# A graph network's edges as one list in units of 17 chunks, instead of 18 padded chunks for each tile

## The chip, the cores and the metric

The kernel runs on one core of one Trainium2 chip. The metric is the device time of one execution in microseconds. Before the change three runs took 12551.64 to 12556.44 us, median 12553.1 us.

Five engines work side by side, each through its own instructions in order: TensorE (PE; its weight loads are PEld), VectorE (DVE), ScalarE (ACT), GpSimd (POOL) and SyncE (SP, which here only starts transfers).

## What is computed

A graph has 12,500 nodes with 128 features each, and 212,500 edges (100,000 pairs in both directions, and one self-loop per node), sorted by their destination `dst`. Four blocks run in turn, each on the normalized and rectified features and each added back to them; cut to what matters:

```
L0: two graph attention convolutions (128 -> 64 -> 128):
    e     = leaky_relu(alpha_src[src] + alpha_dst[dst], 0.2)
    ex    = exp(e - segment_max(e, dst)[dst])
    out   = segment_sum(ex / segment_sum(ex, dst)[dst] * h[src], dst)
L1: a transformer convolution, 8 heads of 16, and a feed-forward part:
    alpha = (q[dst] . k[src]) / sqrt(16)          (per head)
    a     = softmax of alpha over the edges of one dst
    out   = segment_sum(a * v[src], dst) + x @ Wskip, then Wo, norm, 128->512->128, norm
L2: out   = segment_max over the edges of (x[src] @ Ws + edge_weight * ww), then two dense layers
L3: out   = segment mean of h[src]
```

Five of these steps (two in L0, one each in L1, L2, L3) read a row of a table for every edge and reduce over the edges of a node. They are the five edge passes: gat1, gat2, attn, max, sum.

## The kernel before, in words

Nodes are cut into 98 tiles of 128. Each tile owns a padded list of `C = 18` chunks of 128 edges, from the first edge of its first node on; what lies beyond its last node is left out of the sums by its position. A tile that does not fit is flagged and recomputed by a slow loop (`listed`); with these inputs no tile is flagged, and the slow loop runs zero times.

The first stage ("prologue") checks the sorting, loads weights, and prepares the lists: for each tile, three transfers from a row offset held in a register (L339 to L341) fetch 18 x 128 source indices, destinations and weights; `IDX` holds the sources, `first_d` marks where a node's edges begin, `feat_d` and `last_d` hold five rows per tile from which one matrix product gives the squared distance between an edge's destination and each node. Then `before_gat1` makes the first table `t1`. The features stay in SBUF as `X` throughout.

`edge_pass` (L905) runs one pass. `gather` (L858) issues, one tile ahead, 18 indirect transfers on POOL's queue; each fetches 128 table rows into one chunk of a buffer `g` of `G = 6` chunks. A tile part then works in two halves, the second half beside the first half of the next tile, and a `post` generator makes the dense work of a finished tile (`after_gat1` and so on). The generators fix only the order in which the work is written down; a scheduler of the framework then orders each engine's instructions at build time by its own cost estimates, and places the waits.

- `per_node` (L875) and `per_edge` (L885) turn the distances into 0/1 matrices `st` (node by edge) and `se` (edge by node): a product on PE, one ACT instruction over 6 chunks.
- In gat1 and gat2, `st` spreads the node's own term to its edges (L996), `node_max` (L948) finds the maximum over each node's edges by a forward and a backward scan (L961, L965), the rows are multiplied by the exponential (L1024), split into three bf16 parts (`split`, L480: two ACT casts, two DVE subtractions), and summed per node by PE with `se` (`aggregate`, L895).
- In attn, `st` spreads the queries (L1063), DVE multiplies and reduces (L1067, L1070), ACT exponentiates, DVE multiplies the values in place in `g` (L1085), and `aggregate` works in f32.
- In max, PE turns the rows and adds the weight term (L1116, L1120), DVE scans (L1124), PE turns back (L1135), the result is split and summed. In sum the rows go straight into `aggregate`.

PSUM has eight banks: two buffers `big` of two banks each for all one-hot, query, transposed and scanned values, two for `mm`, one each for `ex` and `acc`.

Of the kernel before, what the change touches and what calls it, by code (L numbers as in the profile page):

```python
# [18 lines left out]
N = 12500  # L19
# [12 lines left out]
C = 18  # L32
G = 6
NG = C // G
ET = C * P
GW = G * P

# [5 lines left out]
EP = E + ET + 4  # L43

FE = ET + 2 * P + 1

D3 = 3 * D + 2
GT = 7
XW = D + H
BIG = 1.0e30  # L50
# [6 lines left out]
def gnn_kernel(ctx, tc, a, out):  # L57
# [17 lines left out]
    feat_d = dram.tile([T, 5, ET], BF16, name="feat_d")  # L75
    last_d = dram.tile([T, 5, ET], BF16, name="last_d")
    ewf_d = dram.tile([T, 3, ET], BF16, name="ewf_d")
    first_d = dram.tile([T, FE], BF16, name="first_d")
# [4 lines left out]
    tkv = dram.tile([NP, 2 * D], F32, name="tkv")  # L83
# [22 lines left out]
    X = const.tile([P, T, D], F32, name="X")  # L106
# [4 lines left out]
    IDX = const.tile([P, C, T], I32, name="IDX")  # L111

    FIRST = const.tile([P, C, T], BF16, name="FIRST")
# [74 lines left out]


    V.memset(X[:, T - 1, :], 0.0)  # L190
    x_in = a["x"]
    for t0 in range(0, T - 1, GT):
        t1_ = min(t0 + GT, T - 1)
        SY.dma_start(X[:, t0:t1_, :],
                     x_in[t0 * P:t1_ * P, :].rearrange("(t p) c -> p t c", p=P))
    SY.dma_start(X[:LAST, T - 1, :], x_in[(T - 1) * P:N, :])
# [117 lines left out]
    with tc.tile_pool(name="csr", bufs=1) as cp:  # L314
# [16 lines left out]
        ROWI = cp.tile([1, T1], I32, name="ROWI")  # L331
        V.tensor_copy(ROWI, rowr)


        rs_ = cp.tile([T, ET], F32, name="raw_s")
        rd_ = cp.tile([T, ET + 1], F32, name="raw_d")
        re_ = cp.tile([T, ET], F32, name="raw_e")
        for t in range(T):
            r = nc.values_load(ROWI[0:1, t:t + 1], engines=(SPQ,), min_val=0, max_val=E)  # L339
            for o, s, n in ((rs_, src_e, ET), (rd_, dst_e, ET + 1), (re_, ew_e, ET)):  # L340
                SY.dma_start(o[t:t + 1, :], s[ds(r, n), :].rearrange("n o -> o n"))  # L341
        for c in range(C):
            px = psum([P, P], "mm", "px")
            PE.transpose(px[:, :T], rs_[:, c * P:(c + 1) * P], ident[:T, :T])
            V.tensor_copy(IDX[:, c, :], px[:, :T])
        with tc.tile_pool(name="csr_w", bufs=1) as wp:
            for i, x in enumerate(three(wp, re_, [T, ET], "ew")):
                SY.dma_start(ewf_d[:, i, :], x)


        long_ = cp.tile([T, 1], F32, name="long_")
        tn1 = cp.tile([P, 1], F32, name="tn1")
        V.tensor_scalar_mul(tn1, tn, -1.0)
        with tc.tile_pool(name="csr_d", bufs=1) as dp:
            ch = dp.tile([T, ET + 1], F32, name="ch")
            V.memset(ch[:, 0:1], 1.0)
            V.tensor_tensor(ch[:, 1:], rd_[:, 1:], rd_[:, :ET], ALU.not_equal)
            m = dp.tile([T, FE], BF16, name="m")
            V.memset(m[:, :P], 0.0)
            V.memset(m[:, P + ET + 1:], 0.0)  # L360
            V.tensor_scalar_mul(m[:, P:P + ET + 1], ch, -BIG)
            SY.dma_start(first_d, m)
            for c in range(C):
                pc_ = psum([P, P], "mm", "pc_")
                PE.transpose(pc_[:, :T], ch[:, c * P:(c + 1) * P], ident[:T, :T])
                V.tensor_copy(FIRST[:, c, :], pc_[:, :T])
            o1 = dp.tile([T, ET], BF16, name="o1")
            V.tensor_tensor(o1[:, P:], rd_[:, P:ET], rd_[:, :ET - P], ALU.is_equal)
            V.tensor_reduce(long_, o1[:, P:], AX.X, ALU.max)
            dl = dp.tile([T, ET], F32, name="dl")  # L370
            V.tensor_scalar(dl, rd_[:, :ET], tn1[:T, :], FAR, op0=ALU.add, op1=ALU.min)
            V.memset(o1, 1.0)
            for o in (feat_d, last_d):
                hi, lo = square(dp, dl, [T, ET], "q")
                xb = dp.tile([T, ET], BF16, name="xb")
                V.tensor_copy(xb, dl)
                for k, y in enumerate((o1, o1, xb, hi, lo)):
                    SY.dma_start(o[:, k, :], y)
                if o is feat_d:
                    V.scalar_tensor_tensor(dl, dl, -FAR, ch[:, 1:], op0=ALU.add, op1=ALU.mult)  # L380
                    V.tensor_scalar_add(dl, dl, FAR)
# [7 lines left out]
        V.tensor_scalar(flag, flag, float(ET), None, op0=ALU.is_gt)  # L389
# [72 lines left out]
    def act_norm(t):  # L462
        h = w_([P, D], "hn")
        S.activation(h, X[:, t, :], AF.Relu, bias=NM[:, t:t + 1], scale=RS[:, t:t + 1])
        return h

    def pre(t):
        yield from norm(X[:, t, :], RS[:, t:t + 1], NM[:, t:t + 1])
        return act_norm(t)
# [55 lines left out]
    def run(gens, width):  # L525

        gens, live = list(gens), []
        while gens or live:
            while gens and len(live) < width:
                live.append(gens.pop(0))  # L530
            live = [g for g in live if next(g, live) is not live]


    def before_gat1(t):
        hT = yield from transposed((yield from pre(t)))
        yield from gat_begin(t, hT, w1x, HID, t1)

    run((before_gat1(t) for t in range(T)), 2)
# [9 lines left out]
    def after_gat2(t, r):  # L548
        o = gat_end(r, D, b02)
        V.tensor_add(X[:, t, :], X[:, t, :], o)  # L550
        yield
        hT = yield from transposed((yield from pre(t)))
# [3 lines left out]
        r = w_([P, 3 * D], "qkv")  # L556
        V.tensor_add(r, pm[:, :3 * D], bqkv)
        V.tensor_scalar_mul(r[:, :D], r[:, :D], float(HD) ** -0.5)
        q3 = work.tile([P, 3 * D], BF16, name="q3_")
        split(q3, r[:, :D], D, w_([P, D], "rest"))  # L560
        SY.dma_start(tq[rows(t), :], q3)
        SY.dma_start(tkv[rows(t), :], r[:, D:])

    def after_attn(t, r):
        z = w_([P, H], "zh")
        V.tensor_scalar_add(z, r[:, D:], SM_EPS)
        V.reciprocal(z, z)
        agg = w_([P, D], "agg")
        V.tensor_mul(agg.rearrange("p (h d) -> p h d", h=H),
                     r[:, :D].rearrange("p (h d) -> p h d", h=H),  # L570
                     z.unsqueeze(2).to_broadcast([P, H, HD]))
        hn = act_norm(t)
# [45 lines left out]
        V.tensor_add(X[:, t, :], X[:, t, :], u)  # L618
# [3 lines left out]
        hT = yield from transposed((yield from pre(t)))  # L622
# [7 lines left out]
    def after_max(t, r):  # L630
        hT = yield from transposed(act_norm(t))
# [23 lines left out]
        V.tensor_add(X[:, t, :], X[:, t, :], u)  # L655
        yield
        yield from norm(X[:, t, :], RS[:, t:t + 1], NM[:, t:t + 1])
        h3 = work.tile([P, D3], BF16, name="h3")
        split(h3[:, :3 * D], act_norm(t), D, w_([P, D], "rest"))
# [4 lines left out]
    def after_sum(t, r):  # L664
        z = w_([P, 1], "z")
        V.tensor_scalar_max(z, r[:, D:D + 1], 1.0)
        V.reciprocal(z, z)  # L667
        o = w_([P, D], "o")
        V.scalar_tensor_tensor(o, r[:, :D], z, X[:, t, :], op0=ALU.mult, op1=ALU.add)  # L669
# [8 lines left out]
    def listed(table, c, begin, chunk, wid, ew=False, dt=F32):  # L678


        with tc.tile_pool(name="loop", bufs=1) as lp, tc.tile_pool(name="edge", bufs=1) as ed:
            acc = lp.tile([P, D], F32, name="l_acc")
# [96 lines left out]
    def attn_listed():  # L779
        def begin(t, st):  # L780
# [3 lines left out]
            V.memset(st["s"], 0.0)  # L784
            V.memset(st["m"], -BIG)

            def end():
                V.tensor_copy(st["res"][:, :D], st["acc"])
                V.tensor_copy(st["res"][:, D:], st["s"])
            return end  # L790

        def chunk(g, mk, ng, st):
            m, s, acc, q, ed = st["m"], st["s"], st["acc"], st["q"], st["ed"]
# [16 lines left out]
            cs = ed.tile([P, H], F32, name="csh")  # L810
            V.reduce_sum(cs, over_slots(e), AX.X)
            V.tensor_mul(s, s, corr)
            V.tensor_add(s, s, cs)
            v4 = v.rearrange("p k (h d) -> p k h d", h=H)
            V.tensor_mul(v4, v4, e.unsqueeze(3).to_broadcast([P, K, H, HD]))
            red = ed.tile([P, D], F32, name="red")
            V.reduce_sum(red, over_slots(v), AX.X)
            a3 = acc.rearrange("p (h d) -> p h d", h=H)
            V.tensor_mul(a3, a3, corr.unsqueeze(2).to_broadcast([P, H, HD]))
            V.tensor_add(acc, acc, red)  # L820

        listed(tkv, 2 * D, begin, chunk, XW)

    def plain_listed(table, c, init, ew, chunk):
        def begin(t, st):
            V.memset(st["acc"], init)

            def end():
                V.tensor_copy(st["res"][:, :D], st["acc"])
# [10 lines left out]
    def max_chunk(g, mk, ng, st):  # L840
        acc, ew, ed = st["acc"], st["ew"], st["ed"]
# [8 lines left out]
    def sum_chunk(g, mk, ng, st):  # L850
        acc, ed = st["acc"], st["ed"]
# [6 lines left out]
    def gather(pool, t, table, c, wid, dt):  # L858
        gs = []
        for i in range(NG):  # L860
            g = pool.tile([P, G, wid], dt, name="g", bufs=3 * NG)
            for j in range(G):
                GP.indirect_dma_start(  # L863
                    out=g[:, j, :c], out_offset=None, in_=table,
                    in_offset=bass.IndirectOffsetOnAxis(ap=IDX[:, i * G + j, t:t + 1], axis=0))
            gs.append(g)
        return gs

    def big(name):
        return psum([P, 8, P], "big", name)  # L870


    HALF = ((0, 4), (4, G))

    def per_node(pool, f, i, name, dt=BF16):  # L875

        pm = big("pm_" + name)
        for lo, hi in HALF:
            PE.matmul(pm[:, lo:hi, :].rearrange("p j e -> p (j e)"), NF,  # L879
                      f[:, i * GW + lo * P:i * GW + hi * P], start=True, stop=True)  # L880
        o = pool.tile([P, G, P], dt, name=name)
# [430 lines left out]
```

## Time and profile before

| | us |
|---|---|
| median of three runs | 12553.1 |
| the profiled execution | 12530.6 |
| its span, first to last instruction | 12528.9 |
| POOL busy in it | 8973.4 (72%) |
| PE, DVE, ACT busy | 7534.3, 5793.3, 5340.5 |
| first gather of the pass gat1 | starts at 550.30 |
| first gather of gat2, attn, max, sum | 2851.76, 5427.0, 7976.8, 10308.6 |

Busy time is counted from an engine's own instructions; register, branch and semaphore instructions are not in it. In the groups of instructions a line reads: source line, engine, operation, output <- inputs, shapes, count | busy time in us, mean ns of one | idle time of the engine just before them, and what ended most of it. "issue" there is idle time in which the engine waited for nothing that the profile shows. PEclk is the share of full TensorE clock that was granted.

### The profile page before, as it was taken

What the parts mean: (1) busy time and instruction counts of PE and PEld (TensorE: products, weight loads), DVE (VectorE), ACT (ScalarE), POOL (GpSimd) and SP (SyncE); (2) the same over time, 40 slices, a digit from 0 to 9 for tenths busy, and PEclk for the clock granted to TensorE, in tenths of its full rate; (3) what the DMA queues carried; (4) which work ended last, traced back from release to release, by engine and by line L of the source; (5) the groups of instructions that cost most, each with busy time, mean ns of one, the idle gap of its engine ahead of it and who ended that gap; (6) DMA issues with size and microseconds to landing.
All of it is one profiled execution on the core that took longest, in us unless ns stands there. A gap on an engine that the chain in (4) does not pass through costs nothing. (4 is left out here: it accounts for less than half of the span.)

```text
span 12528.9 us, 142415 instructions
## 1 busy us (share of the span) xinstructions
PE 7534.3 (60%) x43757; PEld 4555.8 (36%) x43758; DVE 5793.3 (46%) x17465; ACT 5340.5 (43%) x10484; POOL 8973.4 (72%) x8835
## 2 busy tenths in 40 slices
PE   0444444444555555568888888777777774444444
PEld 0222222222222222246666666555555541111111
DVE  0634444444555555556666666566666650000000
ACT  0334444444555555556666666444444441111111
POOL 0177777776777777767777777577777767777777
PEclk9999999996555555567777777677777775555555
DMA  2112222222222222233333333334433433333333
GB/s 77 41 34 35 34 35 35 34 34 55 63 63 63 63 63 63 63 86 112 110 107 106 107 108 107 86 111 112 113 111 111 112 94 86 86 86 86 86 86 83
DMA packets 634450, 985.68 MB, mean 79 GB/s; under 512 B 212743, under 2 KB 443939, under 8 KB 633351
## 3 DMA queue, kind: packets, MB, share of 16 engines
q0 software_dynamic: 367008, 756.65, 24.9%
q1 hardware_dynamic: 266660, 219.78, 5.8%
q8 instruction: 346, 5.67, 0.2%
q14 instruction: 436, 3.57, 0.1%
HBM read 902.78 MB, written 73.81 MB: 78 GB/s over the span
## 5 line engine op out<-in xcount | busy, mean ns | idle before, releaser
L863 POOL DMA_INDIRECT g<-t,IDX x3528 | 3687.7, 1045 | 1278.6 <-issue 987.3
L897 PE MATMUL acc<-g,se 128*128 128x136 f32 (+1 forms) x5292 | 1581.9, 411 | 1277.5 <-DMA g<-th,IDX 1141.2
L863 POOL DMA_INDIRECT g<-tkv,IDX x1764 | 1853.2, 1051 | 680.9 <-issue 480.9
L863 POOL DMA_INDIRECT g<-ts__79,IDX x1764 | 1753.9, 994 | 618.1 <-issue 499.3
L892 ACT ACTIVATE se<-pm_se,ones 128x768 bf16<-128x768 f32 (+1 forms) x1470 | 1321.3, 899 | 1925.8 <-PE acc L897 1257.7
L863 POOL DMA_INDIRECT g<-th,IDX x1764 | 1672.7, 948 | 577.9 <-issue 531.9
L897 PEld LDWEIGHTS <-se 128*128 128x128 bf16 x7056 | 835.3, 126 | 2892.6 <-issue 2290.4
L897 PE MATMUL acc<-xs,se 128*128 128x201 bf16 (+1 forms) x3528 | 970.8, 447 | 711.9 <-DVE xs L486 671.0
L890 PE MATMUL pm_se<-NF,f 5*128 5x128 bf16 x8820 | 1119.0, 285 | 74.8 <-DVE fw L961 49.6
L489 DVE TENSOR_TENSOR r<-r 128x128 f32<-128x128 f32 (+2 forms) x392 | 110.6, 282 | 2081.7 <-ACT r L1098 2020.5
L890 PEld LDWEIGHTS <-f 5*128 5x128 bf16 x8820 | 771.5, 124 | 816.3 <-issue 759.7
L993 ACT COPY lg<-g 128x6 f32<-128x6 f32 x588 | 115.6, 205 | 1915.6 <-DMA g<-t,IDX 1865.5
L996 PE MATMUL ex<-ADX,st 128*128 128x6 bf16 x3528 | 189.9, 171 | 1114.3 <-ACT st L882 1114.0
L486 DVE TENSOR_TENSOR xs<-xr,xs 128x402 bf16<-128x402 f32 (+1 forms) x588 | 456.8, 777 | 833.9 <-ACT xs L485 825.3
L882 ACT ACTIVATE st<-pm_st,ones 128x768 bf16<-128x768 f32 x882 | 793.2, 901 | 100.6 <-PE pm_st L879 99.8
L897 PEld LDWEIGHTS acc<-g,se 128*128 128x128 f32 x3528 | 657.3, 270 | 234.5 <-ACT se L892 86.0
L879 PE MATMUL pm_st<-f,NF 5*128 5x512 bf16 x1764 | 688.6, 468 | 78.6 <-DVE g L1067 56.8
L996 PEld LDWEIGHTS <-st 128*128 128x128 bf16 x3528 | 146.3, 107 | 1387.1 <-ACT st L882 1305.8
L1120 PE MATMUL pg<-identb,g 128*128 128x128 bf16 x5292 | 531.9, 255 | 179.5 <-DMA g<-ts__79,IDX 178.2
L897 PE MATMUL acc<-ft,se 128*128 128x386 bf16 x1764 | 506.2, 444 | 169.2 <-DVE ft L486 169.2
L456 ACT ACT_TABLE_LOAD x292 | 374.6, 1283 | 506.4 <-DMA LIST<-list_d 381.2
L484 DVE TENSOR_TENSOR xr<-x,xs 128x402 f32<-128x402 f32 (+1 forms) x588 | 453.6, 771 | 164.0 <-ACT xs L483 156.8
(1095 smaller groups left out, 13885.3 us busy)
## 6 DMA issues: line engine op xcount, KB each, us to landing
g<-t,IDX POOLq DMA_INDIRECT x3528
n<-first_d SPq DMA_DIRECT2D x98, 576.0 KB
g<-tkv,IDX POOLq DMA_INDIRECT x1764
g<-ts__79,IDX POOLq DMA_INDIRECT x1764
g<-th,IDX POOLq DMA_INDIRECT x1764
gt<-gen_d SPq DMA_DIRECT2D x294, 64.5 KB
tkv<-qkv SPq DMA_DIRECT2D x98, 128.0 KB
th<-h SPq DMA_DIRECT2D x98, 96.5 KB
```

The lines of the kernel that those rows point to most:

```text
L456: S.activation(sd, mv[:, 1:2], AF.Sqrt, bias=eps)
L484: V.tensor_tensor(rest, x, a, ALU.subtract)
L486: V.tensor_tensor(c, rest, b, ALU.subtract)
L863: GP.indirect_dma_start(out=g[:, j, :c], out_offset=None, in_=table, in_offset=bass.IndirectOffsetOnAxis(ap=IDX[:, i * G + j, t:t + 1], ax ...
L879: PE.matmul(pm[:, lo:hi, :].rearrange("p j e -> p (j e)"), NF, f[:, i * GW + lo * P:i * GW + hi * P], start=True, stop=True)
L882: S.activation(o, pm[:, :G, :], AF.Relu, scale=-1.0, bias=ones[:, 0:1])
L890: PE.matmul(pm[:, j, :], f[:, e0:e0 + P], NF, start=True, stop=True)
L892: S.activation(o, pm[:, :G, :], AF.Relu, scale=-1.0, bias=ones[:, 0:1])
L897: PE.matmul(acc[:, :wid], lhs[:, j, :], rhs[:, j, :wid], start=(i == 0 and j == 0), stop=(i == NG - 1 and j == G - 1))
L993: S.copy(lg[:, 0, 1 + i * G:1 + (i + 1) * G, :], gs[i][:, :, c + 1:c + 2])
L996: PE.matmul(ex[:, 6 * (i * G + j):6 * (i * G + j) + 6], st[:, j, :], ADX[:, t, :, :].rearrange("p s v -> p (s v)"), start=True, stop=True)
L1120: PE.matmul(pg[:, j, :], gs[i][:, j, k * D:(k + 1) * D], identb, start=False, stop=(j == hi - 1 and k == 2))
```

## The change

The edges are no longer cut by tile. They are one list of `CH = 1661` chunks of 128 (the last one partly padding), in 98 units of `U = 17` (the last has 12). Each chunk is gathered once. A tile sums over a window of 23 chunks: three before its unit, the unit, three after it; the one-hot matrix is zero for edges of other nodes. A tile whose edges leave the window is flagged. The work on edges (`e1`, `e2`) goes by units and the sums (`Pass.tile`) by tiles, as three generators side by side; `e2` of a unit waits for the first group of the next one, since a node's edges can lie in two units.

Buffers and instructions go by groups of three chunks. The 0/1 matrix `st` is made for the unit's own tile and, for the three chunks at each end, for its neighbours' (`spread`). The products of gat1, gat2 and of part of attn, the rests of splits, and the exponentials are written to PSUM (`bank`, `split_in_place`, `p`). PSUM's banks are three `b` of one bank, two `mm`, two `ex`, one `acc`. In attn, chunks 3 to 11 of a unit are summed in f32 as before, the others as three bf16 parts; the table `tkv` has a one behind each head's values, so that the denominators come out of the same sum. The features move from `X` in SBUF to `xd` in DRAM: each post reads its rows and writes them back. The prologue reads the lists by whole rows, in a few transfers.

```diff
-C = 18
-G = 6
...
+CH = (E + P - 1) // P
+U = 17
+GS = 3
+NG = (U + GS - 1) // GS
+WB, WF = 3, 3
+VW = U + WB + WF
+EW = VW * P
...
-        for t in range(T):
-            r = nc.values_load(ROWI[0:1, t:t + 1], engines=(SPQ,), min_val=0, max_val=E)
-            for o, s, n in ((rs_, src_e, ET), (rd_, dst_e, ET + 1), (re_, ew_e, ET)):
-                SY.dma_start(o[t:t + 1, :], s[ds(r, n), :].rearrange("n o -> o n"))
...
+            sd = wp.tile([P, RC * P], F32, name="sd")
+            SY.dma_start(sd, flat(src_e))
...
+            SY.dma_start(rd_[1:, :], bass.AP(at1.tensor, at1.offset, [[U * P, T - 1], [1, EW + 1]]))
...
+    def features(src, t):
+        x = w_([P, D], "x", 3)
+        if src is xd or t < T - 1:
+            SY.dma_start(x, src[rows(t), :])
...
     def after_attn(t, r):
...
+        x = features(xd, t)
...
-        V.tensor_add(X[:, t, :], X[:, t, :], u)
...
+        V.tensor_add(x, x, u)
+        SY.dma_start(xd[rows(t), :], x)
...
+    def gather(pool, u, table, wid, dt, bufs):
         gs = []
...
+        for c, n in groups_of(u):
+            g = pool.tile([P, GS, wid], dt, name="g", bufs=bufs)
+            for j in range(n):
+                k = u * U + c + j
                 GP.indirect_dma_start(
...
-    def big(name):
-        return psum([P, 8, P], "big", name)
...
+    def bank(name):
+        return psum([P, 512], "b", name, 3)
...
+    class Pass:
...
+        def tile(self, t):
+            pool = self.pool
+            f = pool.tile([5, EW], BF16, name="fa")
+            SY.dma_start(f, self.feats[t])
+            yield
+            visits = [w for w in range(VW) if 0 <= t * U + w - WB < CH]
+            acc = psum([P, 512], "acc", "acc", 1)
+            while visits:
...
+                se = per_edge(pool, f, w, n, dt)
+                yield
+                for j in range(n):
+                    k = t * U + w + j - WB
+                    while k not in self.rhs:
+                        yield
+                    x, i = self.rhs[k]
+                    m = x.shape[2]
+                    PE.matmul(acc[:, :m], se[:, j, :], x[:, i, :],
...
+    def edge_pass(name, table, wid, dt, work_of, post):
...
+            lag = 1 if work_of.lookahead else 0
+            for u in range(T + 1 + lag):
+                if u + 1 < T:
+                    gs[u + 1] = gather(pool, u + 1, table, wid, dt, work_of.bufs)
+                live = []
+                if u < T:
+                    live.append(work_of.e1(u, gs[u]))
+                if 0 <= u - lag < T:
+                    live.append(work_of.e2(u - lag, gs[u - lag]))
+                if 0 <= u - lag - 1:
+                    live.append(whole(u - lag - 1))
+                while live or len(posts) > 1:
...
+    def spread(pool, u, f, c, n, each):
...
+        todo = [(u, c, c, n)]
+        if u > 0 and c < WF:
+            todo.append((u - 1, c, U + c, min(n, WF - c)))
+        lo = max(c, U - WB)
+        if u + 1 < T and lo < c + n:
+            todo.append((u + 1, lo, U + WF + lo - (U - WB), c + n - lo))
+        for i, (t, c0, at, m) in enumerate(todo):
+            st = per_node(pool, f, at, m)
...
+    def split_in_place(out, x, w):
...
+        split(out, x, w, x)
...
+    class gat(Pass):
...
+            p = ps_[:, 256:256 + 2 * U].rearrange("p (i c) -> p i c", i=2)
+            S.activation(p[:, :, :n], d[:, :, :n], AF.Exp)
...
+            for i, (c0, m) in enumerate(groups_of(u)):
+                x = bank("x")[:, :m * w].rearrange("p (j c) -> p j c", c=w)
+                V.tensor_mul(x[:, :, :c + 1], gs[i][:, :m, :c + 1],
+                             p[:, 0, c0:c0 + m].unsqueeze(2).to_broadcast([P, m, c + 1]))
+                S.copy(x[:, :, c + 1:], lo[:, c0:c0 + m, :])
+                yield
+                xs = pool.tile([P, GS, 3 * w], BF16, name="xs", bufs=16)
+                split_in_place(xs[:, :m, :], x, w)
...
+    class attn(Pass):
...
+                if self.dtype(c0) is F32:
+                    xs = pool.tile([P, GS, XW], F32, name="xf", bufs=8)
+                    V.tensor_mul(xs[:, :m, :].rearrange("p k (h d) -> p k h d", h=H), v, pi)
+                else:
+                    x = bank("x")[:, :m * XW].rearrange("p (j c) -> p j c", c=XW)
...
+                    split_in_place(xs[:, :m, :], x, XW)
...
+    class maximum(Pass):
...
+                pg = bank("pg")[:, :m * P]
+                PE.matmul(pg, WW, w[:, cols], start=True, stop=False)
...
+                pt = by4("pt_f")
...
+                split_in_place(ft[:, :m, :], pt[:, :m, :], D)
...
```

The buffers of `g` are 18 groups in gat1 and gat2, 17 in attn, 14 in max and 24 in sum; before, nine groups of six chunks.

## The prediction

> **What bounds the kernel now.** I read the page's groups first: four groups of one line, L863, hold all POOL time, and what ends POOL's idle time before them is "issue".
>
> ```profile
> L863 POOL DMA_INDIRECT g<-t,IDX x3528 | 3687.7, 1045 | 1278.6 <-issue 987.3
> L863 POOL DMA_INDIRECT g<-tkv,IDX x1764 | 1853.2, 1051 | 680.9 <-issue 480.9
> L863 POOL DMA_INDIRECT g<-ts__79,IDX x1764 | 1753.9, 994 | 618.1 <-issue 499.3
> L863 POOL DMA_INDIRECT g<-th,IDX x1764 | 1672.7, 948 | 577.9 <-issue 531.9
> ```
>
> These are 5 x 98 x 18 = 8820 gathers. The view of that line gives medians of 944 to 946 ns whatever the row holds (264 to 1024 bytes), and "issue" 2499.3 us over 8201 gaps, 0.305 each. So a gather costs 0.944 + 0.305 = 1.249 us of POOL at least, and a pass of 1764 at least 2203 us.
>
> Second, the windows of the five passes and of a part of the prologue (columns: length, then PE, PEld, DVE, ACT, POOL busy, granted clock, DMA):
>
> ```profile
> 550.00:2803.00 2253.00, 1010.29 (x6398) 599.03 (x6397) 944.10 (x3994) 924.20 (x2199) 1715.11 (x1764) 1.00 0.20 34
> 2851.00:5362.00 2511.00, 1355.79 (x6443) 614.13 (x6444) 1392.83 (x3823) 1410.23 (x2581) 1972.62 (x1764) 0.54 0.27 63
> 5427.00:7896.00 2469.00, 2055.36 (x14250) 1673.72 (x14250) 1597.42 (x4182) 1523.20 (x2940) 1853.19 (x1764) 0.71 0.38 108
> 7976.00:10268.00 2292.00, 1799.84 (x12026) 1172.53 (x12026) 1374.94 (x2784) 956.19 (x1725) 1753.87 (x1764) 0.76 0.40 111
> 10308.00:12519.00 2211.00, 1062.32 (x3525) 330.99 (x3526) 157.01 (x679) 301.88 (x391) 1672.69 (x1764) 0.50 0.34 86
> 450.00:500.00 50.00, 30.15 (x95) 20.75 (x94) 46.91 (x528) 33.36 (x138) 0.00 (x0) 1.00 0.11 23
> ```
>
> The passes (gat1, gat2, attn, max, sum) lie 50, 308, 266, 89 and 8 us over 2203. Of that, POOL busy beyond 1764 x 0.944 = 1665 us makes 50, 307, 188, 89 and 8: gathers that last longer. Attn adds 85 us of POOL waiting for a buffer (releaser ACT g L1081 in the waits). So POOL is the bound in every pass. Why some gathers last longer, the timeline tells:
>
> ```profile
> 4009.76 0.94 POOL L863 DMA_INDIRECT g<-t,IDX  x1 [0.30 <-issue]
> 4021.02 3.27 POOL L863 DMA_INDIRECT g<-t,IDX  x1 [0.30 <-issue]
> 4021.42 0.96 DVE L486 TENSOR_TENSOR xs<-xr,xs 128x786 bf16<-128x786 f32 x1
> 4022.51 0.96 DVE L484 TENSOR_TENSOR xr<-x,xs 128x786 f32<-128x786 f32 x1
> 4023.60 0.66 DVE L965 TENSOR_TENSOR_SCAN bw<-n,fw 18x256 f32<-18x256 bf16 x1
> 4024.60 0.94 POOL L863 DMA_INDIRECT g<-t,IDX  x1 [0.30 <-issue]
> ```
>
> The gather at 4021.02 ends only after three DVE instructions with two inputs in SBUF each; where DVE rests, a gather takes 0.94. Long gathers lie beside L484, L486, L1024 and L1085, all of that kind; L1067, of the same size with one input in PSUM, stands beside hardly any.
>
> Last, the prologue: PE waits once for 206.8 us,
>
> ```profile
> PE px L344 <- DMA raw_s<-src_e: 206.8, 1, 206.8
> ```
>
> while the timeline of SP shows 294 row loads one after the other from 131.51 on.
>
> **The change, part by part**, on the profiled span of 12528.9.
>
> *Gathers.* 1661 chunks a pass instead of 1764: 515 fewer in all, x 1.249 = -643. A pass now needs 1661 x 1.249 = 2075 us, a unit of 17 chunks 21.23.
>
> *Long gathers.* The products and rests go to PSUM, so L484, L486 and L1024 lose their second SBUF input. The backward scan L965 keeps its two; so do the f32 products of attn (9 chunks of 17) and DVE's dense work. The 642 us fall at best to 8 a pass, as in sum (-602), at worst not at all; nearest are the gathers of attn beside the scans, which stay. I keep 15 in gat1, gat2 and max, 70 in attn, 8 in sum: 123, so -519.
>
> *Prologue.* 294 loads (131 to 338) become four of 0.8 to 1.1 MB; the like load of dst at 109.85 landed at about 118.7, so about 9 us each, 36 together: -170. DVE work on 2944 columns instead of 2304: L249 to L381 sum to about 51 us, x 1.28 = +14; the new chunk rows save about what the new comparisons cost. `before_gat1` (395 to 550) is unchanged, its loads of x lie beside it: a first load, 5. Together -150 to -190; I take -170. The 14 loads of X (SP 33.86 to 64) go.
>
> *Ends of passes.* After a pass's last gather come 49, 65, 81, 41 and 11 us (to the next pass's first gather). Now two units of `e2` and two tiles stand behind it where one tile's second half stood: between +5 and +25 each, I take +20, +25, +25, +10, +5 = +85.
>
> *Does the rest keep up with 21.23 us a unit?* This decides. Costs go by instruction size: ACT casts 0.85 us at 786 columns and 0.53 at 402 and started the next instruction about 0.1 earlier, so 0.09 + n/1200; the relu of 768, 0.79, 0.15 + n/1200; DVE 0.07 + n/960 (L1024: 774 columns, next start 0.88 later).
> Gat2, ACT: `st` 23 chunks in 9 pieces 3.8 (before 2.4), `se` 23 in 6 pieces 3.35 (2.4), 12 casts of 393 4.8 (4.5), small copies 1.4 (0.6), two table loads 2.6, the rest 2.0: 18.0, and times 1.04, by which the same sum for before (14.2) misses its measured 14.8 a tile, 18.7, or 88%. DVE: 14.1 (products 2.7, rests 5.5, scans 1.4, the rest as before). PE, at its present 0.54: 23 x 0.33 for the sums, 3.2 `se`, 3 `st`, 1.3 spread, 2.9 the rest: 18.
> Attn, DVE: 20.2 (before 16.7: splits of 8 chunks +2.7, sums and scans in two pieces +0.6), 95%. ACT 18.7: three exponential groups become one, two table loads of four go. PE: 69 products L1063 x 0.076, 9 f32 chunks x 0.38, 14 bf16 x 0.28, 23 `se` x 0.094, `st` 1.8, transposes 1.4, posts 5.5: 23.4 at the present clock 0.71, and 15.4 with the tenth-percentile pitches of the same rows.
> Max: PE 19.5 at its 0.76, DVE 14.9, ACT 10.6. Gat1 (ACT 13) and sum (PE 12) stay under POOL.
> The last window shows how near an engine gets to its limit under this scheduler: DVE 46.91 of 50. So attn's bound is DVE at 20.2/0.94 = 21.5, PE somewhere between 15.4 and 23.4, and three PSUM banks. I take 24.5 us for attn, between the bounds 21.5 and 30 (below), 22.5 for gat2, 22 for max: with 97.7 units 2394, 2198 and 2149, that is 249, 108 and 59 over POOL's 2145, 2090 and 2090: +416.
>
> For PE the clock matters. [...]
> [...] This change has 41 small ACT instructions in gat2 where 18 stood. [...]
> The rows show a fixed part of 0.09 to 0.15 us, and L1067 (one input in PSUM) at 958 ns beside L1085 (both in SBUF) at 954.
>
> *The new wait.* `e2` of a unit starts only when the next unit's first group has landed, three gathers or 3.75 us after its own last one. Behind its copy on ACT are the casts of the unit before, behind its scan on DVE that unit's rests; both have work of 85 to 95% of a unit, so the delay shows as depth, not as rate. A group of `g` must come free before the gather that is three units on (18 buffers of 6 a unit; 17 in attn), and `e2` needs it within two; one unit of 21 us is in hand. I cost it at nothing; the cover is gone where a unit takes longer than 21 us, and then POOL waits, which the 416 counts.
>
> *Transfers.* Posts add at most two on SP a unit, of 0.33 us: 0.7 of 21. A post that waits for its x holds nothing but that post, unless DVE's order puts the add early; the read takes some 2 us of 21. Nothing, and 2 us a unit (+200 a pass) if uncovered.
>
> Sum: 12529 - 643 - 519 - 85 (attn's buffer waits, counted in its 24.5) - 170 + 85 + 416 = 11613. The medians lie 24 above the span (12553.1 against 12528.9): **11640 us**.
>
> **The rivals.**
> *POOL stays the bound everywhere.* Without the 416: 11220. For it: sums of work under 21.23 in all passes but PE in attn by its present clock. Chance 0.27.
> *The three PSUM banks decide, and it is slower.* A unit has 63.7 us of bank time. Pairing each bank's first product with its last reader in attn's trace, `st` held a buffer 3.6 us on average, `se` 3.35, `qe` 3.0, `lt` 3.2. Attn: 9 x 3.6 + 7 x 3.35 + 6 x 3.0 + 4 + three splits of 4.5 (two casts, three DVE, queues between) = 91, over 3 banks 30.4 a unit, 2970; gat2: 9 x 3.6 + 6 x 3.35 + 6 x 4.5 + 3 = 83, 27.6, 2700. With that +825 and +610 replace 249 and 108: 12720. It is slower from a mean of about 26 us a unit over gat2, attn and max. For it: `big` had four banks, and x, held through five instructions on two engines, is new. Against: those holds contain idle waiting; the shortest (1.4, 1.4, 2.2, 2.8) give 52 of 63.7. Chance 0.17.
> *Half of that*, holds or a cold PE: attn 27, gat2 25, max 23: +245 +245 +100, 12230. Chance 0.15.
> *It does not do what it says*: a tile leaves its window and runs the slow loop, some 600 us (3 rounds of 32 to 48 gathers in five passes). Counted on the reference's `dst`, the tightest tiles have 0.36 and 1.09 chunks to spare: none. 0.01.
>
> **How the numbers follow.** Forecast 0.40, the rest as above. 11200 to 12450 leaves out most of the slow rival and a little below. 0.2% (25 us) is about what a measurement of this kernel can tell from none: faster 0.82, same 0.01, slower 0.17.
>
> **What would show it.** Right: 8305 gathers with a mean of about 0.96 us and none of 3; first gather near 380; sum about 2085; POOL's idle time in attn ended by buffers. Wrong: gathers as long as before (then the second input was not it), or POOL waiting in gat2 and max too for `g`, with DVE or PE waiting for readers of a bank `b`.

## The result and the profile after

The changed kernel takes 13521.4 us (median of four runs, 13513.3 to 13524.9) against 12552.4 (12546.9 to 12556.4): a ratio of 1.077, 95% interval 1.075 to 1.079. It is slower by 969 us; 11640 was forecast. The profiled execution took 13513.3 us, its span is 13511.6.

The windows of the five passes, from first to last gather (columns as before: length, then PE, PEld, DVE, ACT, POOL busy, granted clock, DMA share, GB/s):

```profile
429.90:2884.40 2454.50, 1368.12 (x8055) 722.38 (x8055) 1038.18 (x4628) 1287.71 (x4480) 1567.85 (x1661) 0.50 0.16 32
2947.60:5825.20 2877.60, 1712.98 (x8045) 823.49 (x8045) 1443.36 (x4616) 1817.28 (x4941) 1587.13 (x1661) 0.52 0.22 58
5916.80:9073.50 3156.70, 2622.09 (x15932) 1672.26 (x15931) 1956.18 (x5568) 1821.34 (x4241) 1577.39 (x1661) 0.67 0.32 88
9190.50:11355.30 2164.80, 1862.06 (x12341) 1133.90 (x12341) 1417.55 (x3791) 1111.58 (x2649) 1573.86 (x1661) 0.78 0.41 117
11427.60:13503.50 2075.90, 1254.03 (x4484) 445.60 (x4485) 151.61 (x582) 422.60 (x779) 1570.16 (x1661) 0.54 0.34 90
```

POOL is busy 1568 to 1587 us a pass and no longer fills any of the first three, and no other engine does either: 63% ACT at most in gat2, 83% PE in attn. Max and sum, 2165 and 2076, are near what was forecast (2149 and 2083). The groups of the gathers say the same:

```profile
L934 POOL DMA_INDIRECT g<-t,IDX x3322 | 3155.0, 950 | 2416.3 <-issue 751.6
L934 POOL DMA_INDIRECT g<-tkv,IDX x1661 | 1577.4, 950 | 1670.8 <-DVE x L1294 1089.7
```

A gather takes 950 ns on average where it took 1045 (gat1 and gat2) and 1051 (attn): the long ones are gone. The time went into waiting, once or twice a unit. The timeline of POOL in gat2 shows how: the 17 gathers of a unit run with one short pause (1.14 us after the third), and before the next unit's first gather stands a long one:

```profile
4303.00 0.94 POOL L934 DMA_INDIRECT g<-t,IDX  x1 [0.30 <-issue]
4311.70 0.94 POOL L934 DMA_INDIRECT g<-t,IDX  x1 [7.76 <-ACT tp L511]
```

Per unit, by the median distance of the first gathers of neighbouring units (units 20 to 90), gat1 takes 25.37 us, gat2 29.82, attn 32.98, max 22.36, sum 21.25; POOL needs 21.23.

### The profile page after: what moved, and what is told of

The parts are those of the page before. It is cut to its first block, busy times and chain, and to the rows that moved or that the text cites. A ratio compares the mean times of both kernels' runs of the same rounds, so it can differ in the third digit from the quotient of the medians.

```text
span 13511.6 us, 169563 instructions
## 1 busy us (share of the span) xinstructions
PE 9169.7 (68%) x50504; PEld 5011.7 (37%) x50505; DVE 6424.3 (48%) x21435; ACT 6755.2 (50%) x17972; POOL 7883.1 (58%) x8320
## 5 line engine op out<-in xcount | busy, mean ns | idle before, releaser
L1021 PE MATMUL acc<-xs,se 128*128 128x201 bf16 (+3 forms) x8090 | 2452.0, 440 | 988.2 <-ACT se L948 971.7
L948 ACT ACTIVATE se<-pm_se,ones 128x512 bf16<-128x512 f32 (+2 forms) x2729 | 1798.0, 663 | 2329.9 <-PE pm_se L962 1255.7
L962 PE MATMUL pm_se<-NF,fa 5*128 5x128 bf16 x11215 | 1632.8, 275 | 191.7 <-ACT r L1350 100.6
L948 ACT ACTIVATE st<-pm_st,ones 128x384 bf16<-128x384 f32 (+2 forms) x2631 | 1399.1, 532 | 460.4 <-PE pm_st L954 450.0
L1021 PE MATMUL acc<-g,se 128*128 128x386 bf16 x2243 | 938.2, 490 | 718.5 <-DMA g<-th,IDX 711.3
L954 PE MATMUL pm_st<-fe,NF 5*128 5x384 bf16 (+2 forms) x2631 | 1134.1, 432 | 420.5 <-DVE xs L521 142.3
L962 PEld LDWEIGHTS <-fa 5*128 5x128 bf16 x11215 | 886.1, 114 | 1382.3 <-issue 1251.1
L1154 ACT COPY lg<-g 128x3 f32<-128x3 f32 (+1 forms) x1172 | 229.4, 196 | 1608.1 <-DMA g<-t,IDX 1557.9
L519 DVE TENSOR_TENSOR x<-x,xs 128x201 f32<-128x201 f32 (+5 forms) x1464 | 688.4, 470 | 545.4 <-ACT xs L518 522.3
L1257 PE MATMUL qe<-q,st 128*128 128x128 bf16 x6729 | 841.2, 287 | 143.1 <-ACT st L948 136.0
L521 DVE TENSOR_TENSOR xs<-x,xs 128x201 bf16<-128x201 f32 (+5 forms) x1464 | 681.5, 466 | 370.6 <-ACT xs L520 360.0
L1158 PEld LDWEIGHTS <-st 128*128 128x128 bf16 x4486 | 375.6, 122 | 1187.4 <-ACT st L948 958.7
L1257 PEld LDWEIGHTS <-st 128*128 128x128 bf16 x6729 | 630.3, 130 | 427.8 <-ACT st L948 325.5
```

The costliest lines, as they stand in the source:

```text
L519: V.tensor_tensor(rest, x, a, ALU.subtract)
L521: V.tensor_tensor(c, rest, b, ALU.subtract)
L948: S.activation(o[:, :n, :], pm[:, :n, :], AF.Relu, scale=-1.0, bias=ones[:, 0:1])
L954: PE.matmul(pm[:, :n, :].rearrange("p j e -> p (j e)"), NF, f[:, c * P:(c + n) * P], start=True, stop=True)
L962: PE.matmul(pm[:, j, :], f[:, (c + j) * P:(c + j + 1) * P], NF, start=True, stop=True)
L1021: PE.matmul(acc[:, :m], se[:, j, :], x[:, i, :], start=(j == 0 and w == max(0, WB - t * U)), stop=(j == n - 1 and n == len(visits)))
```

## The experiments

**What the trace suggested for gat1 and gat2.** The timeline of all engines in gat2, from the landing of the unit being gathered to the next unit's first gather:

```profile
4332.59 0.94 POOL L934 DMA_INDIRECT g<-t,IDX  x1 [0.30 <-issue]
...
4333.78 0.20 ACT L1154 COPY lg<-g 128x3 f32<-128x3 f32 x1 [4.04 <-DMA g<-t,IDX]
4333.88 0.68 ACT L948 ACTIVATE se<-pm_se,ones 128x512 bf16<-128x512 f32 x1
...
4334.62 1.49 PE L1021 MATMUL acc<-xs,se 128*128 128x393 bf16 x4 [3.73 <-ACT se L948]
4335.11 0.19 ACT L1154 COPY lg<-g 128x2 f32<-128x2 f32 x1
...
4336.10 0.28 PE L1134 MATMUL pbx<-ident,bw 17*128 17x17 f32 x1
...
4336.42 0.17 DVE L1183 TENSOR_TENSOR ml<-am,pbx 128x17 f32<-128x17 f32 x1 [3.89 <-PE pbx L1134]
...
4340.92 0.20 ACT L1193 ACTIVATE pbx<-d 128x34 f32<-128x34 f32 x1
...
4341.34 0.57 DVE L1203 TENSOR_TENSOR x<-g,pbx 128x387 f32<-128x387 f32 x1
...
4342.67 0.94 POOL L934 DMA_INDIRECT g<-t,IDX  x1 [9.13 <-ACT tp L511]
```

The copies L1154 at 4333.78 and 4335.11 need rows of the unit that POOL is gathering at that moment. The exponential L1193 behind them belongs to the unit two before it, and its inputs do not need those rows; it stands behind them because the scheduler put them first on ACT (and `pbx` on PE stands behind `acc`, which waits for the `se` behind the copy). The product x at 4341.34 frees the first buffer for the gather at 4342.67. (The view puts that wait down to `tp` L511, which only happened to end in between: the first gather of a unit starts 0.76 us after the end of the first product of the unit three before it, in the median of gat1 and of gat2.) So a loop closes: gather 17 chunks, land, copy, exponential, product, buffer, gather: in the median 23.6 us from a unit's first gather to its last copy and 6.2 from there to the next unit, 29.8 in all. Theory A is this loop; theory B says that the first product comes too late (75 us after the unit's first gather in gat1, 88 in gat2, where before it was 63 in both) for three units of buffers; theory C is the rival of the prediction, three PSUM banks. For attn, where ACT hardly waits for rows, C stands against theory D, the work of TensorE at its clock of 0.67. Runs e1 to e4 were made to tell them apart; e1, e2 and e4 touch gat1 and gat2 alone, e3 attn alone.

**e1.** Fewer buffers, not more:

```
-        lg = pool.tile([P, k, g + 2, h], F32, name="lg", bufs=3)
+        lg = pool.tile([P, k, g + 2, h], F32, name="lg", bufs=3 if k > 1 else 2)
```

> Edit: in gat1 and gat2 the logits `lg` have two buffers instead of three; the 18 buffers of `g` and the three banks `b` stay. Theory A, the order on ScalarE: in the changed kernel all six copies of the logits of the unit just being gathered stand ahead of the exponential of the unit two before it, so that a loop closes: gather (17 x 1.25) -> landing -> last copy, 23.6 us after the unit's first gather -> exponential -> product -> buffer of `g` -> next unit's first gather, 29.8 us in gat2 (25.4 in gat1, where five copies stand ahead). With two buffers only the first copy can stand ahead, and the loop is 5 + 6 us: gat1 21.3 to 22.5 us a unit, gat2 22 to 25, the whole 12500 to 12950. Theory B, depth: the first product comes 75 (gat1) and 88 us (gat2) after the unit's first gather, and three units of buffers give a third of that; 18 buffers stay, so nothing changes: 13520 within 60. Theory C, three PSUM banks `b`: nothing changes, 13520 within 60.

Measured: 12694.2 us, 827 less; gat1 21.32 a unit, gat2 24.64, in the ranges of A. B and C alone, which had no change, are out.

```profile
431.20:2516.40 2085.20, 1337.13 (x8100) 749.52 (x8100) 1046.30 (x4652) 1315.54 (x4495) 1577.64 (x1661) 1.00 0.22 37
2568.40:4995.20 2426.80, 1666.34 (x8047) 800.00 (x8047) 1426.81 (x4623) 1802.80 (x4938) 1581.71 (x1661) 0.56 0.28 68
```

Gat1 went from 2454.5 to 2085.2 us with about the same busy time on every engine (PE 31 us less, ACT 28 more); POOL's floor is 2075. The order on ACT, in its timeline in gat2, is now one copy, exponential, the other copies:

```profile
3518.86 0.19 ACT L1154 COPY lg<-g 128x3 f32<-128x3 f32 x1
...
3523.86 0.20 ACT L1193 ACTIVATE pbx<-d 128x34 f32<-128x34 f32 x1
...
3525.86 0.20 ACT L1154 COPY lg<-g 128x3 f32<-128x3 f32 x1
3526.33 0.21 ACT L1154 COPY lg<-g 128x3 f32<-128x3 f32 x1
```

**e2.** `feats, lookahead, bufs = feat_d, True, 24` instead of 18.

> Edit: `g` in gat1 and gat2 has 24 buffers instead of 18, four units instead of three. Theory A, the order on ScalarE: the order that is built with it also has one copy only ahead of the exponential, so the gain is the same as with two buffers of `lg`: gat1 21.3 to 22.5 us a unit, gat2 22 to 25, the whole 12500 to 12950. Theory B, depth: 75/4 = 18.8 and 88/4 = 22.1, so gat1 is at POOL's 21.3 and gat2 at 22.1: about 12370 to 12500. Theory C, three PSUM banks: gat1 and gat2 stay at 25.4 and 29.8, 13520 within 60.

Measured: 12801.1; gat1 22.64, just above A's 22.5, and gat2 24.64, as A has it. In gat2 one copy stands ahead of the exponential in this build; in gat1 two in one half of the units and five in the other. The first product came later than in the changed kernel, 85 and 98 us after the unit's first gather: added depth was filled, and B's 22.1 was not reached in gat2.

**e3.** `x = psum([P, 512], "ex", "x")` instead of `bank("x")` in attn.

> Edit: in attn the products x are written to the two banks `ex` (where only the exponentials are in that pass) instead of the three banks `b`; nothing else. Theory C, the banks: x takes three of some 28 uses of `b` in a unit of attn and holds them longest, so the 33.0 us a unit fall to 29 to 31, attn by 200 to 390 us. Theory D, TensorE's work: its 27.6 us a unit at a granted clock of 0.67 and its waits for ScalarE's 0/1 matrices set the unit, so attn changes by less than 60 us. Gat1 and gat2 stay in both.

Measured: 13306.1; attn 2928.8 us, 29.53 a unit, 228 us less, where C had it. PE's busy time fell too, with as many products, and the granted clock was 0.71 instead of 0.67, so the run is no clean price of the banks:

```profile
5930.30:8859.10 2928.80, 2460.07 (x15953) 1664.64 (x15953) 1923.94 (x5567) 1745.98 (x4244) 1575.76 (x1661) 0.71 0.35 95
```

**e4.** `x = pool.tile([P, GS, w], F32, name="x", bufs=4)` instead of `bank("x")` in gat1 and gat2.

> Edit: in gat1 and gat2 the products x and the rests of their splits are in SBUF again, in four buffers, as before the change; the rest of the change stays. The prediction's step on long gathers: the subtractions of the splits have two SBUF inputs again, so gathers of 3 us come back in gat2, some 100 to 250 us over the 944 ns each. Theory C, the banks: six of 22 uses of `b` a unit go, so gat2 gains more than it loses, 29.8 to 26 to 28 us a unit. Theory A, the order on ScalarE: two copies of the unit being gathered stand ahead of the exponential, one of them of the second group; the loop is 9 + 6 us and POOL decides: gat1 22 to 23, gat2 24 to 26 us a unit.

Measured: 12400.5, below the kernel before on the same chip (12526.8); gat1 21.49, gat2 22.29, below what A and C each allowed, and POOL never waited for a buffer in either. It does not tell the two apart: x is gone from the banks, and the order is another one too (in gat2, in half of the units two copies of the unit two on stand ahead of the exponential, in the others none, instead of six). It does say that, as built, the PSUM part of the change costs more in gat2 than it brings:

```profile
2565.70:4733.10 2167.40, 1564.54 (x8089) 738.17 (x8088) 1435.61 (x4646) 1766.44 (x4953) 1661.44 (x1661) 0.62 0.32 77
```

The long gathers that come back are 95 us over 944 ns each, against 21 in the changed kernel. That is less than was expected here, and none of 3 us is among them: the longest takes 1.34 us, where the kernel before had 3.59.

**e5 to e8.** Each changed one thing alone or together: one bf16 part of the queries (e5), attn in f32 (e6), the parts of e10 below (e7), the rests in SBUF with e1's edit (e8). On the chip where these four ran the kernel before took 16123 us, and they took 16413, 16794, 16719 and 17091, all longer than it. In the pass sum of e7, ACT alone waited 1189 us for something that the profile does not tell. What slowed that chip is not known, so these times are not used for or against a theory. Their edits were run again: e5 and e8 together as e9, e7 (with e6 in it) as e10.

**e9.** In gat1 and gat2 the edit of e1 and `split(xs, x, w, pool.tile([P, GS, w], F32, name="xr"))` in place of `split_in_place`; in attn one product with `q[:, 0:D]` in place of three.

> Edit: in gat1 and gat2 two buffers of `lg`, x in a bank `b` and the rests of the splits in SBUF; in attn the queries are spread by one of their three bf16 parts (46 of 69 products of a unit are left out, the result is less exact). Gat2, theory C (banks): x holds its bank half as long, 24.6 falls to 22 to 23.3 us a unit; theory D (work and order): 24 to 25. Attn, theory D (TensorE's work at its low clock sets the unit): 33.0 falls to 27.5 to 29.5; theory C: at most 1.8 us less, 31.2 to 33.

Measured: 12361.1; gat2 23.76 a unit, between the two theories (24.64 in e1); attn 30.71, 2934 us, also between: 46 products left out brought 2.3 us, not 4.9 (granted clock 0.64 instead of 0.67).

**e10.** e1's edit; e4's in gat2 only; and attn in f32:

```
-        WHOLE = range(GS, U - WB - (U - WB) % GS)
+        WHOLE = range(U)
...
-            r = yield from summed(self.pool, acc, XW)
+            r = self.pool.tile([P, XW], F32, name="r")
+            S.copy(r, acc[:, :XW])
```

with 20 buffers of `xf` instead of 8.

> Edit: two buffers of `lg` in gat1 and gat2; products x and rests in SBUF in gat2 only; attn all in f32 with 20 buffers of `xf`, no splits and no x in `b`. Gat1 2085 us, gat2 2140 to 2210 with 80 to 120 us of long gathers. Attn: theory C 28 to 29.5 us a unit; theory D 31 to 32; both 27 to 28.5. The whole 11950 to 12250.

Measured: 11832.9, against 12525.3 for the kernel before. Gat1 2085, gat2 2165 (92 us of long gathers), attn 2602.7 or 27.07 a unit, at the lower end of "both". The whole is 117 us below the range.

**e11 and e12.** `WB, WF = 2, 3` on the best parts: e11 with attn as in e3, e12 with attn in f32.

> Edit: as the best parts, but attn keeps its bf16 chunks, with x in the banks `ex`; and the window is two chunks before the unit instead of three, which still holds every tile's edges (1.09 chunks were to spare at that end): 22 chunks summed instead of 23, and in attn 12 chunks in f32 and 5 in three bf16 parts instead of 9 and 8. Attn: 29.5 us a unit with x in `ex`; one of 23 chunks less on TensorE (1.2 us) and one split of three less (1 us on ScalarE, 1 on VectorE): 27 to 29. Gat1 and gat2 at POOL's 21.3 and 22.3; max 10 to 60 us shorter. The whole 11850 to 12200.

> Edit: as the best parts (attn all in f32), with the window of 22 chunks. Attn: a chunk less on TensorE for the queries, the 0/1 matrices and the sums, about 1.2 us of a unit less than with 23 chunks if TensorE sets the unit, nothing if POOL's buffers or the banks do. The whole 20 to 150 us below the best parts.

Measured: 11959.4 and 11936.4. Gat1 and gat2 gained 11 and 30 us on e10 and attn stayed (27.03 and 27.31 a unit), but max grew from 2180 to 2319 and 2302, so that e12 is 104 us slower than e10 where 20 to 150 less were expected. In max PE had fewer products and yet was busy longer, 2020 and 2000 us instead of 1880, at a granted clock of 0.69 and 0.70 instead of 0.77; POOL's waits for its products (`pg`) rose from 121 to 273 us in e11. In attn of e12 it was the same in small: 4% fewer products, 2220 us busy instead of 2214, clock 0.80 instead of 0.87. Why the clock fell is open.

**e13 to e15.** What makes attn's 27 us? e13 is e10 with e9's edit of the queries, e14 is e10 with 21 buffers of `g` and 16 of `xf` in attn, e15 is e10 again, timed four times.

> Edit: the best parts (attn in f32), and the queries are spread by one bf16 part of three (the result is less exact). No split and no x is left in attn, and the banks `b` are held 48% of the time only. Theory D, TensorE's work: 46 of 69 products, 46 x 0.09 = 4.1 us, go, and 27.1 us a unit fall to 22.5 to 24. Theory C, the banks: the queries' bank is held some 0.9 us shorter, six a unit over three banks: 25.5 to 27. Theory B, depth: 27.1 stays.

> Edit: the best parts, and in attn 21 instead of 17 buffers of `g` (and 16 of `xf` instead of 20, which still hold more than two units). Theory B, depth: 17 buffers are 2.83 units and 21 are 3.5, so 27.1 falls to 22. Theories C and D: the buffers only wait longer, full, for the engines: 26.5 to 27.3 us a unit, the first product of a unit later by most of what was added.

> The best parts once more, with an interval: 11833 us was seen, a ratio to the kernel before of 0.9447; 0.942 to 0.948.

Measured: e14 11823.8, 27.09 a unit, while attn's first product moved from 78 to 97 us after the unit's first gather: depth is not it. e15 11823.1 (11815.4 to 11853.5), a ratio of 0.944 (0.9425 to 0.9457): the version that beats both kernels (not on the chip of e5 to e8, where the same edits, as e7, took 3.7% longer than the kernel before). e13 took 11914.5: attn became slower, 27.89 a unit, with two thirds of the queries' products gone. D and C both missed, and B, which had it unchanged, falls with e14. The rows of PE, by form (count | busy, mean ns of one), in e10 and then in e13:

```profile
L1021 PE MATMUL acc<-xf,sef 128*128 128x136 f32 x4342 | 782.0, 324 | 100.5 <-ACT sef L948 99.3 <-DVE xf L1294 0.4
L1260 PE MATMUL qe<-q,st 128*128 128x128 bf16 x6633 | 651.3, 244 | 202.3 <-ACT st L948 189.3 <-DVE lg L1267 5.9 <-DVE st L477 2.9
```
```profile
L1021 PE MATMUL acc<-xf,sef 128*128 128x136 f32 x4334 | 931.1, 357 | 208.0 <-DVE mv L479 150.4 <-ACT sef L948 43.7 <-DVE xf L1292 3.3
L1259 PE MATMUL qe<-q,st 128*128 128x128 bf16 x2211 | 340.1, 279 | 81.6 <-ACT st L948 78.0 <-DVE g L1263 2.3 <-DVE lg L1102 1.2
```

The queries lost 311 us, but the same sums took 149 us more, and the other larger rows of PE 7 to 52 us more each; the windows of attn in e10 and e13 show why, a granted clock of 0.87 and of 0.67, and PE busy 2214 and 2309 us:

```profile
4798.30:7401.00 2602.70, 2214.41 (x17308) 1695.56 (x17308) 1604.39 (x4824) 1563.90 (x3592) 1592.63 (x1661) 0.87 0.39 106
```
```profile
4793.50:7482.40 2688.90, 2309.47 (x12862) 1678.88 (x12861) 1568.37 (x4817) 1569.72 (x3585) 1576.13 (x1661) 0.67 0.38 103
```

So in attn PE's time is no sum of fixed prices. One can also follow each wait back to what ended it, from the first gather of unit 90 to that of unit 20, and add up which engine was being waited for. In attn PE holds 18.6 of 33.0 us a unit in the changed kernel, 16.4 of 27.1 in e10 and 22.8 of 27.9 in e13, and POOL next to none. In gat2 POOL and the landing of its rows hold about a third of the 29.8 in the changed kernel, as the loop has it, and none in e1, where ACT has 11.0 and PE 10.5.

## Why the prediction was wrong

By the terms of its sum, on the span (12528.9 to 13511.6, +983):

| term | forecast | measured |
|---|---|---|
| 515 gathers fewer | -643 | -643 (8305 gathers) |
| long gathers | -519 | about -600 (1.7, 21, 10, 6.6, 2.9 left) |
| attn's buffer waits, counted anew in the last line | -85 | -85 |
| prologue | -170 | -120 (first gather 429.9 instead of 550.3) |
| ends of passes | +85 | +105 (+14, +26, +36, +31, -2) |
| the rest cannot keep up | +416 | about +2320 |

The last line is POOL's gaps of over 0.4 us (409, 841, 1102, 98 and 0 in the five passes) less the 0.305 us of issue in each of the 415. Pass by pass, from first to last gather, the forecast was short by 364 us in gat1 (2090), 680 in gat2 (2198), 763 in attn (2394) and 16 in max.

**The gathers.** The long ones went, more of them than was taken: gat2's mean is 956 ns. But only a part is shown to come from the second SBUF input. Where e4 puts x and the rests back into SBUF, 95 us stand in gat2 instead of 21, of the 307 before the change; no run shows what saved the rest. One rival is that the DVE instructions are shorter now: the subtractions of the split (L519, L521) cover 393 columns in 0.57 us where L484 and L486 covered 786 in 0.97. In attn 9 us are left and not 70: the prediction gave the f32 products two SBUF inputs, but they read the exponentials from PSUM (`xf<-g,pbx`). In the kernel before, 230 of the 371 gathers that ran beside L1085 (for more than 0.15 us) lasted over 1.05 us, and of the 369 beside L1067 none.

**The prologue** missed 50 us of its 170: I had put 9 us for each of the four loads, and DVE waited 33.7 us for `dd` and 45.0 for `raw_d`.

**The step that failed is "Does the rest keep up with 21.23 us a unit?", and in it "The new wait": "the delay shows as depth, not as rate. ... I cost it at nothing".** Its sums of work for gat2 were right: ACT 18.6 us busy a unit (18.7 forecast), PE 17.5 (18), DVE 14.8 (14.1). They did not decide. With `e2` a unit later, the exponential of a unit falls, in the order of ACT, behind the copies of the logits of the unit being gathered, and an instruction that waits for POOL then stands ahead of the one that POOL waits for. In the kernel before the same copies waited for the same rows (885 us in gat2), but POOL never waited for a buffer there. e1 takes the loop away, with nearly the same work on every engine: 369 us in gat1, all that the forecast was short there, and 451 of the 680 in gat2. "Depth" was the wrong picture: one buffer fewer of `lg` cured it, and six more of `g` helped by the other order that was built with them.

**The banks.** What was left in gat2, 24.64 a unit, went to 23.76 with the rests and to 22.27 with x and rests in SBUF; attn lost 3.4 us with x in other banks. That is the direction of the rival with 0.17, but not its sum: the holds, measured as it measured them, fill about three quarters of the three banks' time in gat2 and six tenths in attn, not all. Each of these edits also changes the order that is built, so how much is bank and how much is order is not settled.

**Attn.** This is the other term that was mis-sized: I took 24.5 us a unit between PE's 15.4, from the tenth-percentile pitches, and 23.4 at its row's 0.71 (the "cold PE" of the rivals), and it took 33.0. PE was busy 26.8 of them at 0.67: the starts of the queries' products lay 95 ns apart on average, not 76, those of the bf16 sums 306, not 280. And an engine need not reach the 94% that I read from DVE in the prologue: PE is the largest holder of the chain here while it is busy 83% of the time (85% in e10, 86% in e13). That PE could come near the 15.4 was my estimate, and no run shows it: PE's busy share was 83% before and after, it worked 26.8 us a unit instead of 21.0, and the clock went from 0.71 to 0.67. How the missing 8.5 us divide between the banks, the clock and the order is not settled.

**The rivals.** Slower was right at 0.17, by a time outside the range (12450) and beyond that rival (12720); gat1, which it left alone, lost 202 us against before, by the loop. So the chance on the sign was no insight into the cause. The signs for "wrong" came true in one half: POOL waits for `g` in gat2, but with no gathers of 3 us, and in max hardly (98 us).

## What to carry to other kernels

Where engines run in order and a scheduler writes the order, sums of work per engine give a floor, not a time: look on each engine for an instruction that waits for the gathered data and stands ahead of one on which the gather's buffers depend, and add up that loop (here landing, copy, exponential, product). A buffer fewer for the small tile that is written early can be worth more than buffers for the large one (12694 us in e1, 12801 in e2). And price PE by what it does in the trace at its clock, do not expect it to reach 94% busy (here it already set the pace at 83 to 86%), and do not count on a gain in clock (attn went from 0.71 to 0.67) or on a linear saving (e13 has two thirds of the queries' products less than e10 and took 0.8 us a unit more).

## What the runs showed of the hardware that was not expected

TensorE's granted clock did not follow its busy share: in attn 0.67 at 83% busy (changed kernel), 0.87 at 85% (e10), 0.67 at 86% (e13). In e3 it stayed at half for 20 us of nearly full work, and then rose; the two windows are of attn:

```profile
7500.00:7520.00 20.00, 18.46 (x94) 13.26 (x94) 10.86 (x30) 8.01 (x22) 9.04 (x10) 0.50 0.33 90
7520.00:7524.00 4.00, 3.76 (x36) 3.19 (x36) 1.57 (x7) 3.12 (x7) 0.00 (x0) 0.94 0.03 11
```

The longest idle time of PE in those 20 us was 0.62. What grants the clock, here and in e10, stays open.

The column itself can mislead: gat1 shows 1.00 in the kernel before and in e1 and 0.50 in the changed kernel, while the same sum takes 369, 367 and 367 ns there (kernel before, e1, changed kernel), and the products of `pm_se` (5 x 128, bf16) start 107, 106 and 106 ns after one another. Two groups, from 1000 to 2000 us of the kernel before and of the changed one:

```profile
L897 PE MATMUL acc<-xs,se 128*128 128x201 bf16 x780 | 154.0, 369 | 101.0 <-DVE xs L486 90.4 <-ACT se L892 10.6
```
```profile
L1021 PE MATMUL acc<-xs,se 128*128 128x201 bf16 x900 | 201.2, 367 | 148.5 <-ACT se L948 148.5
```

In attn of e10 these starts lie 106 ns apart where the record has 0.50, and 56 where it has 1.00; in attn of the kernel before, 107 and 56. So the 1.00 of gat1 in the kernel before was no full clock; the trace holds no clock record there before 2904 us.
